# Two PSUM banks per tile in a product-quantised residual block: wider evacuations, moved norms, one-operand VectorE steps

## The chip, the cores and the metric

One core of a Trainium2 chip runs the whole kernel in one launch. The metric is the device time in microseconds; a kernel's time is the median of its runs. The engines are TensorE (PE in the profile, its weight loads PEld), VectorE (DVE), ScalarE (ACT), GpSimd (POOL) and SyncE (SP, which here only issues DMAs).

## The reference

A residual block over x of shape (16, 256, 28, 28), all float32. Two "convolutions" replace the product of patches and weights by a soft look-up: each channel's 3×3 patch is compared with 16 centroids, and the softmax of the negative distances weights a table.

```python
def amm_conv3x3(x, centroids, w_sub):              # centroids (256, 16, 9), w_sub (256, 9, 256)
    patches = conv_general_dilated_patches(x, (3, 3), (1, 1), 'SAME')
    p = patches.reshape(B, C, 9, H*W).transpose(0, 3, 1, 2)
    d = sum(p*p) - 2*einsum('bncs,cks->bnck', p, centroids) + sum(centroids*centroids)
    attn = softmax(-d, axis=-1)
    lut = einsum('cks,cso->cko', centroids, w_sub)
    return einsum('bnck,cko->bno', attn, lut)      # then back to (B, 256, 28, 28)

h = groupnorm(x)                                   # 32 groups
out = relu(bn1(amm_conv3x3(h, centroids1, wsub1)))
out = bn2(amm_conv3x3(out, centroids2, wsub2))
out = out * sigmoid(relu(mean(out) @ w1 + b1) @ w2 + b2)
return x + relu(out + h)
```

## The kernel before

The work is cut into 128 blocks: 2 layers × 16 images × 4 (half of the input channels, half of the image's rows). A block has 128 channels and N = 392 positions. For each block there are these steps:

- `patches` (L338) fetches shifted rows from DRAM (`home1`, `home2`) into the tiles `pt`.
- `logits` (L352), four times (`mm` 0 to 3), computes the scores: 16 small matmuls of 32×32 into four PSUM tiles `lg`, one for each row of the array's 32-row groups (`i`), four column groups in each.
- `exps` (L366) takes exp(2·score) out of PSUM on ScalarE into the tile `e`. In layer 1 the first group of half the blocks goes a longer way (`wide_copy` and what follows), which subtracts the maximum first.
- `num_b` (L412) makes the denominators and the ninth numerator in PSUM (`nb`); `split_b` (ScalarE) and `join_b` (VectorE) take them out, `recip_dve` inverts, `spread` shuffles the reciprocals to where they are needed (`rb`).
- `num_a` (L399), four times, makes the other numerators (`na`, one PSUM tile for each of two row halves `r`). For `mm` 0 and 1 `copy_a` (ScalarE) copies them to SBUF and `scale_q` (GpSimd) scales them there; for `mm` 2 and 3 `scale_a` (VectorE) scales them out of PSUM.
- `product` (L482) multiplies the nine scaled numerators `q` of a block by a weight tile into the accumulator `acc`. A Strassen-like scheme gets the 2×2 block product of an image from seven products; `mix` (GpSimd) forms differences of numerators, `acc_copy`, `acc_add` and `reg_add` assemble the four outputs.
- `norm_out` or `norm_both` applies batch norm on ScalarE; layer 0's result is scattered to DRAM (`to_home2`), layer 1's goes through the gate (`se_hidden`, `se_gate`) and the `finish_` steps to the output.

Nothing is left to a scheduler. Every call is entered by hand with `at(cluster, sub, f, ...)`; the program issues them in order of (cluster, sub), and each engine runs its own in that order. A block starts every two clusters, so an even cluster holds scores (sub 0.1 and 0.2), denominators (1.3), two groups of numerators (1.35) and a product (2.0); an odd one holds scores, two groups of numerators (1.0) and a product. An image takes eight clusters.

```python
at(g + p, 0.1 + 0.1 * q, logits, u, mm)
at(g + p, 0.12 + 0.1 * q, exps, u, mm)
at(g + 2, 1.4, split_b, u)
at(g + 2, 1.45, copy_a, u, mm)
at(g + 12, 0.0, acc_add, l, b, c11, (n, 11))
```

All PSUM tiles share one ring, `p_ring`: eight slots of one bank (512 float32 in each partition). `bank(name)` takes a slot; whoever takes it next waits until all readers of its last owner are done.

Beside the main path some preparation runs once. Group norm of the next image is `gn_stats`, `gn_mean` (with L305, a squaring of two columns), `gn_var` and `gn_apply`. For image 0 the channels of layer 1 are ranked: `code_spread` (L573), `rank_score` (L593), `rank_keep` (L597, which writes 128 scores of 4 bytes each to DRAM), `rank_row`, `rank_make` (L609) and `rank_look`.

Of the kernel before, what the change touches and what calls it, by code (L numbers as in the profile page):

```python
# [17 lines left out]
P = 128  # L18
# [5 lines left out]
N = RT * W  # L24
# [43 lines left out]
def kernel(  # L68
# [28 lines left out]
    p_ring = ctx.enter_context(tc.tile_pool(name="p_ring", bufs=8, space=PSUM))  # L97
# [4 lines left out]

    def bank(name):
        return p_ring.tile([P, 512], F32, tag="ps", name=name)
# [190 lines left out]
    def gn_mean(b, k0=0, n=NB):  # L295
# [9 lines left out]
        nc.vector.tensor_mul(dv[:, :n], dv[:, :n], dv[:, :n])  # L305
# [46 lines left out]
    def logits(u, mm):  # L352
        bs = []
        for i in range(4):
            bk = bank("lg")
# [7 lines left out]
            bs.append(bk)  # L363
        u["lg", mm] = bs

    def exps(u, mm):  # L366
        eg = epool.tile([P, 4, N], F32, tag="e", name="e")
        for i, bk in enumerate(u.pop(("lg", mm))):
            nc.scalar.activation(eg[:, i, :], bk[:, :N], AF.Exp, scale=2.0)  # L369
        u["e", mm] = eg  # L370

    def wide_copy(u, mm):
        eg = epool.tile([P, 4, N], F32, tag="e", name="e")
        for i, bk in enumerate(u.pop(("lg", mm))):
            nc.scalar.copy(eg[:, i, :], bk[:, :N])  # L375
# [23 lines left out]
    def num_a(u, mm):  # L399
        bs = [bank("na") for _ in range(2)]  # L400
        es = u["e", mm]
        for i in range(4):
            for r in range(2):
                nc.tensor.matmul(  # L404
                    bs[r][32 * i : 32 * i + 32, :N],
# [6 lines left out]
    def num_b(u):  # L412
        bs = [bank("nb") for _ in range(2)]
        for mm in range(4):
            es = u["e", mm]
            for i in range(4):
                for r in range(2):
                    nc.tensor.matmul(  # L418
                        bs[r][32 * i : 32 * i + 32, :N],
# [6 lines left out]
    def split_b(u):  # L426
        b0, _ = u["nb"]
# [7 lines left out]
    def join_b(u):  # L435
        _, b1 = u.pop("nb")
# [32 lines left out]
    def copy_a(u, mm):  # L469
        for r, bk in enumerate(u.pop(("na", mm))):  # L470
            u["q", 2 * mm + r] = pair(u, mm)[:, r, :]
            nc.scalar.copy(u["q", 2 * mm + r], bk[:, :N])  # L472

    def scale_a(u, mm):
        rb = u.pop(("rb", mm))
        for r, bk in enumerate(u.pop(("na", mm))):
            u["q", 2 * mm + r] = pair(u, mm)[:, r, :]
            nc.vector.tensor_mul(u["q", 2 * mm + r], bk[:, :N], rb[:, r, :])  # L478
# [94 lines left out]
    def code_spread(o):  # L573
# [8 lines left out]
        nc.vector.tensor_max(csum[:, o : o + 1], csum[:, o : o + 1], m2)  # L582
# [10 lines left out]
    def rank_score(o):  # L593
        nc.vector.tensor_reduce(score[:, o : o + 1], hpads[o], axis=AX.X, op=ALU.max)
        nc.vector.tensor_mul(score[:, o : o + 1], score[:, o : o + 1], posn[:, o : o + 1])

    def rank_keep(o):  # L597
        nc.sync.dma_start(view(d_sc, o * P, [[1, P], [1, 1]]), score[:, o : o + 1])
# [10 lines left out]
    def rank_make(o):  # L609
        row = idx["row"]  # L610
        eq, gt = row[:, 768:1024], row[:, 1024:1280]
        s = score[:, o : o + 1]
        nc.vector.scalar_tensor_tensor(
            eq, row[:, :C], s, row[:, C * (1 + o) : C * (2 + o)], op0=ALU.is_equal, op1=ALU.mult
        )
        nc.vector.scalar_tensor_tensor(gt, row[:, :C], s, eq, op0=ALU.is_gt, op1=ALU.add)
# [286 lines left out]
    for l in range(2):  # L903
        for b in range(B):
# [22 lines left out]
            if l == 0 or b == B - 1:  # L927
                at(g + 11, 1.9, norm_out, l, b, *c12)
                at(g + 11, 1.91, norm_out, l, b, *c22)
                at(g + 12, 0.3, norm_out, l, b, *c11)  # L930
                at(g + 13, 0.3, norm_out, l, b, *c21)
            else:
                for o in range(NB):
                    at(g + 12 + o, 0.3, norm_both, b, o)
            if l == 0:
                for o in range(2):
                    if b == 0:
                        at(g + 12 + o, 0.35, rank_score, o)
# [268 lines left out]
```

## Time and profile before

| | |
|---|---|
| median of 3 runs | 2728.22 us (2721.29 to 2731.6) |
| the profiled execution | 2732.52 us, its span 2731.0 us |
| mean granted TensorE clock | 0.995 |
| PE busy | 2663.6 us (98%), 36984 matmul records |
| VectorE, ScalarE, GpSimd busy | 1718.3, 1445.9, 2075.3 us |
| exps L369 | 1920 of 128×392, 528 ns each |
| copies L472, scalings L478 | 512 each of 128×392, 513 and 554 ns |

A float32 matmul shows as two matmul records and two weight loads. In a line of the profile L369 is line 369 of the kernel; `e<-lg` names the tiles written and read. A timeline line gives start, duration, engine, line, operation, tiles, count and, in brackets, how long the engine stood idle before it and who ended that. The ends of matmuls are modelled, so stages are read from start to start.

### The profile page before, as it was taken

What the parts mean: (1) busy time and instruction counts of PE and PEld (TensorE: products, weight loads), DVE (VectorE), ACT (ScalarE), POOL (GpSimd) and SP (SyncE); (2) the same over time, 40 slices, a digit from 0 to 9 for tenths busy, and PEclk for the clock granted to TensorE, in tenths of its full rate; (3) what the DMA queues carried; (4) which work ended last, traced back from release to release, by engine and by line L of the source; (5) the groups of instructions that cost most, each with busy time, mean ns of one, the idle gap of its engine ahead of it and who ended that gap; (6) DMA issues with size and microseconds to landing.
All of it is one profiled execution on the core that took longest, in us unless ns stands there. A gap on an engine that the chain in (4) does not pass through costs nothing. (4 is left out here: it accounts for less than half of the span.)

```text
span 2731.0 us, 87796 instructions
## 1 busy us (share of the span) xinstructions
PE 2663.6 (98%) x36984; PEld 1293.3 (47%) x36984; DVE 1718.3 (63%) x3943; ACT 1445.9 (53%) x3233; POOL 2075.3 (76%) x1425
## 2 busy tenths in 40 slices
PE   5899999999999999999999999999999999999998
PEld 2444544444444444444444444444444444444444
DVE  4765655566565556655567766666766676766674
ACT  3445444544445554555545555656556656556653
POOL 4856787766887677876678887788887788887787
PEclk9999999999999999999999999999999999999999
DMA  9665667766566666666585555545555445555441
GB/s 198 150 143 159 144 156 197 190 148 129 151 163 160 172 155 140 172 166 160 127 180 119 106 121 121 115 102 116 115 122 125 111 105 115 115 124 125 110 105 57
DMA packets 223624, 374.50 MB, mean 137 GB/s; under 512 B 30633, under 2 KB 194009, under 8 KB 223225
## 3 DMA queue, kind: packets, MB, share of 16 engines
q1 hardware_dynamic: 216280, 334.87, 53.3%
q0 software_dynamic: 6944, 33.95, 3.7%
q8 instruction: 295, 4.83, 0.8%
q14 instruction: 105, 0.85, 0.1%
HBM read 288.93 MB, written 79.80 MB: 135 GB/s over the span
## 5 line engine op out<-in xcount | busy, mean ns | idle before, releaser
L369 ACT ACTIVATE e<-lg 128x392 f32<-128x392 f32 x1920 | 778.2, 528 | 803.9 <-PE lg L357 797.7
L495 POOL TENSOR_TENSOR qp<-qp,qp 128x784 f32<-128x784 f32 x512 | 938.2, 1861 | 26.0 <-DVE qp L478 26.0
L486 PE MATMUL acc<-qp,w_S 128*128 128x392 f32 x2048 | 704.4, 494 | 0.9 <-POOL qp L495 0.9
L467 POOL TENSOR_TENSOR qp<-qp,rb 128x784 f32<-128x784 f32 x256 | 471.5, 1859 | 181.3 <-DVE rb L459 173.5
L357 PE MATMUL lg<-pt,wd 32*32 32x392 f32 x16384 | 541.2, 504 | 21.1 <-DMA pt<-home 16.2
L459 DVE STREAM_SHUFFLE rb<-r 128x392 f32<-128x392 f32 x1024 | 551.7, 603 | 0.0
L486 PEld LDWEIGHTS acc<-qp,w_S 128*128 128x128 f32 x2048 | 386.7, 190 | 299.1 <-issue 17.4
L486 PE MATMUL acc<-qp,w_A 128*128 128x392 f32 x1536 | 521.2, 492 | 0.0
L438 DVE SCALAR_TENSOR_TENSOR r<-nb,kst,r 128x392 f32<-128x392 f32 x128 | 79.8, 624 | 572.9 <-ACT r L429 557.6
L404 PE MATMUL na<-e,cwa 64*32 64x392 f32 x8192 | 412.1, 495 | 9.0 <-issue 9.0
L486 PEld LDWEIGHTS acc<-qp,w_A 128*128 128x128 f32 x1536 | 291.8, 190 | 213.8
L418 PE MATMUL nb<-e,cwb 64*32 64x392 f32 x8192 | 373.8, 496 | 3.9 <-issue 3.4
L467 POOL TENSOR_TENSOR qo<-qo,rb 128x392 f32<-128x392 f32 x128 | 131.0, 1024 | 301.6 <-DVE rb L455 301.4
L357 PEld LDWEIGHTS lg<-pt,wd 32*32 32x32 f32 x16384 | 232.8, 103 | 257.3 <-issue 170.9
L444 DVE RECIPROCAL r<-r 128x392 f32<-128x392 f32 x128 | 331.9, 2593 | 0.0
L478 DVE TENSOR_TENSOR qp<-na,rb 128x392 f32<-128x392 f32 x512 | 253.3, 554 | 68.4 <-PE na L404 58.9
L404 PEld LDWEIGHTS na<-e,cwa 64*32 64x32 f32 x8192 | 147.0, 106 | 236.4 <-ACT e L369 122.0
L418 PEld LDWEIGHTS nb<-e,cwb 64*32 64x32 f32 x8192 | 144.1, 107 | 226.2 <-issue 140.5
L472 ACT COPY qp<-na 128x392 f32<-128x392 f32 x512 | 211.8, 513 | 9.1 <-PE na L404 9.1
L429 ACT ACTIVATE r<-nb,kst 128x392 f32<-128x392 f32 x128 | 87.6, 684 | 105.6 <-PE nb L418 100.8
L375 ACT COPY e<-lg 128x392 f32<-128x392 f32 x128 | 52.9, 501 | 149.8 <-PE lg L357 149.8
L493 POOL TENSOR_TENSOR qo<-qo,qo 128x392 f32<-128x392 f32 x128 | 130.8, 1022 | 1.7
(149 smaller groups left out, 1747.9 us busy)
## 6 DMA issues: line engine op xcount, KB each, us to landing
pt<-home SPq DMA_DIRECT2D x768, 209.0 KB
pt<-home SPq DMA_DIRECT2D x756, 104.5 KB
home<-xpad SPq DMA_DIRECT2D x31, 899.0 KB
xt<-in_x SPq DMA_DIRECT2D x30, 784.0 KB
out_dram<-y SPq DMA_DIRECT2D x32, 392.0 KB
w_S<-d_wS SPq DMA_DIRECT2D x4, 576.0 KB
st<-in_wsub SPq DMA_DIRECT2D x4, 512.0 KB
st<-d_wa SPq DMA_DIRECT2D x16, 128.0 KB
```

Of the source, the lines that this page charges most:

```text
L357: nc.tensor.matmul(bk[32 * c : 32 * c + 32, :N].rearrange("p (r w) -> p r w", w=W), lhsT=wts["wd", u["hh"]][32 * i : 32 * i + 32, mm, c, : ...
L369: nc.scalar.activation(eg[:, i, :], bk[:, :N], AF.Exp, scale=2.0)
L404: nc.tensor.matmul(bs[r][32 * i : 32 * i + 32, :N], lhsT=wts["cwa", u["hh"]][64 * r : 64 * r + 64, mm, i, :], rhs=es[64 * r : 64 * r + 64, ...
L418: nc.tensor.matmul(bs[r][32 * i : 32 * i + 32, :N], lhsT=wts["cwb", u["hh"]][64 * r : 64 * r + 64, mm, i, :], rhs=es[64 * r : 64 * r + 64, ...
L444: nc.vector.reciprocal(u["r"], u["r"])
L459: nc.vector.stream_shuffle(rb[:, r, :], u["r"], mask_of(2 * mm + r))
L467: nc.gpsimd.tensor_tensor(q, q, u.pop(("rb", mm)), ALU.mult)
L472: nc.scalar.copy(u["q", 2 * mm + r], bk[:, :N])
L478: nc.vector.tensor_mul(u["q", 2 * mm + r], bk[:, :N], rb[:, r, :])
L486: nc.tensor.matmul(accs[key][:, :N], lhsT=wl[w][:, k, :], rhs=us["q", k], start=first and n == 0, stop=last and n == len(ks) - 1,)
L493: nc.gpsimd.tensor_tensor(out_u["q", 8], in0["q", 8], in1["q", 8], ALU.subtract)
L495: nc.gpsimd.tensor_tensor(pair(out_u, mm), pair(in0, mm), pair(in1, mm), ALU.subtract)
```

## The change

- The ring has four slots of two banks. `banks(name)` gives both banks as a [128, 2, 512] tile; `bank(name)` gives the first of a slot's two.
- The scores of two rows `i` share a slot, as do the two halves of numerators and of denominators. `exps`, `wide_copy`, `copy_a` and `scale_a` read both banks in one instruction of 784 columns.
- On ScalarE the batch norm of the first half of channels (`norm_out` of c11, `norm_both` of half 0) moves from sub 0.3 to 1.46 of its cluster, and `finish_relu` from 0.9 to 1.46: behind `copy_a` (1.45). What follows image 0's norm (`rank_score`, `rank_keep`, `h0_keep`) moves to 1.91 to 1.93.
- Small VectorE operations of two tensors become operations of one tensor and a per-partition scalar (L305, column by column; L582; L595). `rank_make` compares on VectorE and multiplies and adds on GpSimd; its sum becomes `rank_sum`, a cluster later.
- The score column is copied to 32 columns and transposed in 32×32 blocks, so that `rank_keep` writes four pieces of 128 bytes.

```diff
-    p_ring = ctx.enter_context(tc.tile_pool(name="p_ring", bufs=8, space=PSUM))
+    p_ring = ctx.enter_context(tc.tile_pool(name="p_ring", bufs=4, space=PSUM))
+    def banks(name):
+        return p_ring.tile([P, 2, 512], F32, tag="ps", name=name)
     def bank(name):
-        return p_ring.tile([P, 512], F32, tag="ps", name=name)
+        return banks(name)[:, 0, :]
...
-        nc.vector.tensor_mul(dv[:, :n], dv[:, :n], dv[:, :n])
+        for i in range(n):
+            nc.vector.tensor_scalar_mul(dv[:, i : i + 1], dv[:, i : i + 1], dv[:, i : i + 1])
...
         for i in range(4):
-            bk = bank("lg")
+            if i % 2 == 0:
+                bs.append(banks("lg"))
+            bk = bs[-1][:, i % 2, :]
...
         for i, bk in enumerate(u.pop(("lg", mm))):
-            nc.scalar.activation(eg[:, i, :], bk[:, :N], AF.Exp, scale=2.0)
+            nc.scalar.activation(eg[:, 2 * i : 2 * i + 2, :], bk[:, :, :N], AF.Exp, scale=2.0)
...
-        bs = [bank("na") for _ in range(2)]
+        bs = banks("na")
...
-                    bs[r][32 * i : 32 * i + 32, :N],
+                    bs[32 * i : 32 * i + 32, r, :N],
...
-        bs = [bank("nb") for _ in range(2)]
+        bs = banks("nb")
...
-            nc.scalar.copy(u["q", 2 * mm + r], bk[:, :N])
+        nc.scalar.copy(pair(u, mm), u.pop(("na", mm))[:, :, :N])
...
-            nc.vector.tensor_mul(u["q", 2 * mm + r], bk[:, :N], rb[:, r, :])
+        nc.vector.tensor_mul(pair(u, mm), u.pop(("na", mm))[:, :, :N], rb)
...
-        nc.vector.tensor_max(csum[:, o : o + 1], csum[:, o : o + 1], m2)
+        nc.vector.tensor_scalar_max(csum[:, o : o + 1], csum[:, o : o + 1], m2[:, 0:1])
...
-        nc.vector.tensor_mul(score[:, o : o + 1], score[:, o : o + 1], posn[:, o : o + 1])
+        nc.vector.tensor_scalar_mul(score[:, o : o + 1], score[:, o : o + 1], posn[:, o : o + 1])
+        wide = small.tile([P, 32], F32, name="score_w")
+        nc.vector.tensor_copy(wide, score[:, o : o + 1].to_broadcast([P, 32]))
+        turned = small.tile([P, 32], F32, name="score_t")
+        nc.vector.transpose(turned, wide)
+        idx["turned", o] = turned
     def rank_keep(o):
-        nc.sync.dma_start(view(d_sc, o * P, [[1, P], [1, 1]]), score[:, o : o + 1])
+        nc.sync.dma_start(view(d_sc, o * P, [[32, 4], [1, 32]]), idx["turned", o][::32, :])
...
-        nc.vector.scalar_tensor_tensor(
-            eq, row[:, :C], s, row[:, C * (1 + o) : C * (2 + o)], op0=ALU.is_equal, op1=ALU.mult
-        )
-        nc.vector.scalar_tensor_tensor(gt, row[:, :C], s, eq, op0=ALU.is_gt, op1=ALU.add)
+        nc.vector.tensor_scalar(eq, row[:, :C], s, None, op0=ALU.is_equal)
+        nc.vector.tensor_scalar(gt, row[:, :C], s, None, op0=ALU.is_gt)
+        nc.gpsimd.tensor_tensor(eq, eq, row[:, C * (1 + o) : C * (2 + o)], ALU.mult)
+        nc.gpsimd.tensor_tensor(gt, gt, eq, ALU.add)
+    def rank_sum(o):
...
-                at(g + 12, 0.3, norm_out, l, b, *c11)
+                at(g + 12, 1.46, norm_out, l, b, *c11)
...
-                    at(g + 12 + o, 0.3, norm_both, b, o)
+                    at(g + 12 + o, 0.3 if o else 1.46, norm_both, b, o)
...
-                        at(g + 12 + o, 0.35, rank_score, o)
-                        at(g + 12 + o, 0.6, rank_keep, o)
-                        at(g + 12 + 2 * o, 0.65, h0_keep, o)
+                        at(g + 12 + o, 0.35 if o else 1.91, rank_score, o)
+                        at(g + 12 + o, 0.6 if o else 1.92, rank_keep, o)
+                        at(g + 12 + 2 * o, 0.65 if o else 1.93, h0_keep, o)
...
-                        at(g + 20, 0.9, finish_relu, b, q)
+                        at(g + 20, 1.46, finish_relu, b, q)
...
         at(15 + o, 1.9, rank_make, o)
+        at(16 + o, 1.7, rank_sum, o)
```

More of the change, by code (lines that the diff above doesn't have):

```diff
@@ L362, in logits @@
                 )
-            bs.append(bk)
         u["lg", mm] = bs
@@ L374, in wide_copy @@
         for i, bk in enumerate(u.pop(("lg", mm))):
-            nc.scalar.copy(eg[:, i, :], bk[:, :N])
+            nc.scalar.copy(eg[:, 2 * i : 2 * i + 2, :], bk[:, :, :N])
         u["e", mm] = eg
@@ L418, in num_b @@
                     nc.tensor.matmul(
-                        bs[r][32 * i : 32 * i + 32, :N],
+                        bs[32 * i : 32 * i + 32, r, :N],
                         lhsT=wts["cwb", u["hh"]][64 * r : 64 * r + 64, mm, i, :],
@@ L426, in split_b @@
     def split_b(u):
-        b0, _ = u["nb"]
+        b0 = u["nb"][:, 0]
         r = rpool.tile([P, N], F32, tag="r", name="r")
@@ L435, in join_b @@
     def join_b(u):
-        _, b1 = u.pop("nb")
+        b1 = u.pop("nb")[:, 1]
         r, q, w = u["r"], u["q", 8], u["w"]
@@ L469, in copy_a @@
     def copy_a(u, mm):
-        for r, bk in enumerate(u.pop(("na", mm))):
+        for r in range(2):
             u["q", 2 * mm + r] = pair(u, mm)[:, r, :]
-            nc.scalar.copy(u["q", 2 * mm + r], bk[:, :N])
+        nc.scalar.copy(pair(u, mm), u.pop(("na", mm))[:, :, :N])
     def scale_a(u, mm):
         rb = u.pop(("rb", mm))
-        for r, bk in enumerate(u.pop(("na", mm))):
+        for r in range(2):
             u["q", 2 * mm + r] = pair(u, mm)[:, r, :]
-            nc.vector.tensor_mul(u["q", 2 * mm + r], bk[:, :N], rb[:, r, :])
+        nc.vector.tensor_mul(pair(u, mm), u.pop(("na", mm))[:, :, :N], rb)
     accs = {}
@@ L610, in rank_make @@
         row = idx["row"]
-        eq, gt = row[:, 768:1024], row[:, 1024:1280]
+        eq, gt = row[:, 768:1024], (row[:, 1024:1280] if o else row[:, 1280:1536])
         s = score[:, o : o + 1]
-        nc.vector.scalar_tensor_tensor(
-            eq, row[:, :C], s, row[:, C * (1 + o) : C * (2 + o)], op0=ALU.is_equal, op1=ALU.mult
-        )
-        nc.vector.scalar_tensor_tensor(gt, row[:, :C], s, eq, op0=ALU.is_gt, op1=ALU.add)
+        nc.vector.tensor_scalar(eq, row[:, :C], s, None, op0=ALU.is_equal)
[3 more added lines that the diff above has]
+    def rank_sum(o):
+        gt = idx["row"][:, 1024:1280] if o else idx["row"][:, 1280:1536]
         rf = small.tile([P, 1], F32, name="rf")
```

## The prediction

> **What bounds the kernel now.** I read the page first (part 1), then the waits, then the timeline of two late stretches of work, then the tiles that the diff names.
>
> ```profile
> PE 2663.6 (98%) x36984; PEld 1293.3 (47%) x36984; DVE 1718.3 (63%) x3943; ACT 1445.9 (53%) x3233; POOL 2075.3 (76%) x1425
> ...
> L369 ACT ACTIVATE e<-lg 128x392 f32<-128x392 f32 x1920 | 778.2, 528 | 803.9 <-PE lg L357 797.7
> ```
>
> TensorE is busy 98% of the span; everything else has room. ACT's large idle time ahead of the exps (L369) is ACT waiting for TensorE, so it costs nothing as such. Only time that TensorE loses inside its stages can be won. The timeline shows how much that is. First a short ("odd") cluster of image work in layer 1, then the numerators of a long ("even") one:
>
> ```profile
> 1789.97 2.03 PE L357 MATMUL lg<-pt,wd 32*32 32x392 f32 x64
> ...
> 1790.65 0.63 PEld L357 LDWEIGHTS lg<-pt,wd 32*32 32x32 f32 x31 [0.23 <-issue]
> 1790.95 3.23 ACT L369 ACTIVATE e<-lg 128x392 f32<-128x392 f32 x8 [5.49 <-PE lg L357]
> ...
> 1791.92 1.64 PE L404 MATMUL na<-e,cwa 64*32 64x392 f32 x32
> ...
> 1792.28 0.10 PEld L404 LDWEIGHTS na<-e,cwa 64*32 64x32 f32 x1 [0.18 <-ACT e L369]
> 1792.61 0.24 PEld L404 LDWEIGHTS na<-e,cwa 64*32 64x32 f32 x15 [0.22 <-issue]
> ...
> 1793.49 0.93 PE L486 MATMUL acc<-qo,w_S 128*128 128x392 f32 x2
> ```
>
> ```profile
> 1782.39 1.52 PE L404 MATMUL na<-e,cwa 64*32 64x392 f32 x32
> ...
> 1783.84 0.93 PE L486 MATMUL acc<-qo,w_S 128*128 128x392 f32 x2
> ```
>
> Read start to start. The scores (L357) take 1.95 us in both kinds of cluster (1789.97 to 1791.92). The numerators (L404) take 1.57 us in the odd one (to 1793.49), 1.45 in the even one (1782.39 to 1783.84), for the same 32 matmul records. Product and denominators repeat to the hundredth (6.12 and 2.66 us). So two small losses recur in every cluster. **The second half of the scores** is issued slowly: the records of the first 16 matmuls lie 7 ns apart, those of the second 17 ns, with about 42 ns wherever the next PSUM bank starts, where a load carries a wait for that bank and the matmul before it a signal. Three such steps at 25 ns extra are 0.075 us. **The odd numerators** wait for ACT:
>
> ```profile
> PEld na L404 <- ACT e L369: 122.0, 357, 0.6
> PEld nb L418 <- ACT e L369: 61.7, 94, 1.3
> ```
>
> 357 weight loads of L404 have ACT's exp as their last releaser; the ring hands them the banks that the exps have just read. Most of the 122 us is the change of stage in any case; what the wait really costs is the difference of 1.57 and 1.45.
>
> In layer 0 there is a third loss. The score matmuls need the bank of the last product, which VectorE's addition (L523) releases, and now and then a tiny operation stands before it:
>
> ```profile
> 403.78 2.14 DVE L305 TENSOR_TENSOR gn_dv<-gn_dv 128x2 f32<-128x2 f32 x1
> 404.02 1.86 POOL L467 TENSOR_TENSOR qp<-qp,rb 128x784 f32<-128x784 f32 x1
> ...
> 405.84 0.55 DVE L523 TENSOR_TENSOR hpad<-acc,hpad 128x392 f32<-128x392 f32 x1
> ...
> 406.54 0.53 PE L357 MATMUL lg<-pt,wd 32*32 32x392 f32 x4 [1.15 <-DVE hpad L523]
> ```
>
> A multiplication of two columns takes 2.14 us while POOL runs; the last four score matmuls start at 406.54. By tile it takes 159/300/2139 ns (min/median/max) over 17, and L582, on one column, 1355 and 6711 ns.
>
> [...] L305 and L582 (two SBUF inputs) stretch, L304 (one from PSUM) stays at 145 to 147 ns. [...] the trace has 528 on average and 497 at the start of this stage. [...]
>
> **The change, part by part.**
>
> *Ring.* Eight one-bank slots become four of two banks; `acc`, `gnp`, `sep`, `sqp` now hold a whole one. Counted in order of release, the even cluster's scores get the slots of lg, na, na, acc, the odd one's na, na, nb, acc; numerators and denominators get slots of scores in the same cluster. These are the owners of before, within one bank. One shift: the third row of scores waits for `acc` too, not only the fourth. L523 ends 0.67 us after the scores start, that row goes at 1.04, so nothing is lost, except in the one cluster of eight with two L523 first: some 0.03 us × 32 = +1.0.
>
> *Exps.* 1920 of 392 columns become 960 of 784. The 784-wide forms in the trace (907 ns from SBUF, L805) read SBUF; with two pointer operands 784 columns (L550, 1101) cost 327 more than 392 (L537, 774), which is 0.833 per column. So I add 327 to 497 and take **D = 0.824 us**; bounds 0.80 and 0.91 (L805). It starts 0.027 later, when the second bank is done: 1.015 us after the scores begin, ends at 1.84, seen by TensorE some 0.05 later at 1.89. Before, the second bank came at 1.87 + 0.05. The next starts 0.70 later (0.653 of streaming and the 0.05 that separates exps now) and is seen at 2.61, against 2.71 for the fourth bank before.
>
> *Score issue.* Of three steps inside the second half one stays: 2 × 25 ns = 0.050 us off the stage, ending at 1.905; bounds 0 (the steps are no matter of waits) and 0.06. The first exp (1.89) is just ahead, so it does not eat this. 222 clusters (256 less the 32 above and the first two) × 0.050 = **-11.1**.
>
> *Odd numerators.* The second pair could start 0.68 after the first, at 2.59, and gets its slot at 2.61. Now its first half starts at 2.64, its second at 2.71; with both at 2.61 the last record, and the product with it, comes 0.084 earlier, of which 0.050 is counted: 0.034 × 94 clusters (one odd cluster in four waits little now) = **-3.2**; bounds 0 and -8.
>
> *Numerators' copies and scalings* (L472, L478) go from 512 to 256 each. VectorE: 2 × 0.495 busy becomes about 0.82 + 0.09; 256 × 0.08 = 20 us off an engine that is not the bound: 0, covered by the 6.12 us product.
>
> *Small VectorE operations.* L305 as two operations with a pointer scalar at about 0.17 (L584, 174 ns) costs 0.3, like its undisturbed self, and L582 0.17. What TensorE lost behind them: stretches of 1.97, 1.05, 1.5 and 0.7 us (L305, near 404, 574, 661 and 491 us), 1.7 and 0.7 (L582), 2.1 (L616 near 204 us, whose 256-wide comparison is split, half of it to POOL). That is 9.7; some will turn into other small waits and the wide comparisons may still meet POOL, so I take **-8**; bounds -10 and -3.
>
> *Ranks.* Four POOL operations of about 0.7 us (L752) once. `rank_sum`, which waits for them, stands on VectorE a cluster later, ahead of the spreads of sub 1.8; POOL is past them by then: 0. Score copy and transposition add about 0.3 us to VectorE twice, in slack before L523: 0. The 128 four-byte pieces become four of 128 bytes: SP holds one issue either way, now behind the patches of cluster 12; d_h0's store follows it there. The next patches wait for TensorE anyway ("SPq L343 <- PE lg" is SP's longest wait): 0, bounds -2 and +2.
>
> *Norms and Relu on ACT* move behind the numerators' copies. Now L537 and L550 fill ACT's gap between exps and L429; there no score or product of that cluster or the next is late. Moved, the norm ends near 8.5 us of the 12.2 us cluster, before POOL, at about 11, issues the scatter that reads it; L808 and the store follow a cluster later. 0; if POOL came early, up to 0.8 us × 15 images of waiting in its queue, with the scalings behind it, +3 at most on TensorE.
>
> Sum: +1.0 - 11.1 - 3.2 - 8 = **-21.3**. The profiled execution took 2732.5 us (span 2731.0), 4.3 above the median of 2728.2; it should come to 2711, and the median to 2707.
>
> **Rivals.** *A, nothing in the steady clusters:* signals, not waits, set the issue steps and stay, or the scores end on something else. Then only the small operations pay: 2720. For it: the steps show wait and signal at the same place. Against: in layer 0 clusters with one more semaphore instruction the stage is 0.024 longer. *B, slower:* the wide exp holds two banks until its end, and the denominators and numerators queue behind it. With D = 1.0 the first slot comes at 1.015 + 1.0 + 0.05 = 2.065, 0.11 us behind today's 1.956 in every cluster, the second one at 1.015 + 0.88 + 1.05 = 2.945, in odd clusters 0.22 behind today's (two halves at once allowed for): 128 × 0.11 + 128 × 0.22 = 42, less 8: 2762. It decides from D = 0.915 on (loss 9, about what the small operations win); over 0.95 it is slower by more than 0.5%. For it: L805's 907. Against: PSUM sources are quicker (684 against 774 ns, both with two pointers, L429 and L537). *C, chance in the early part:* from 26 to 342 us TensorE idles 23 us, L404's loads up to 4.8 us at once on "issue", near 16 KB fetches of instructions while the homes are written. A shifted program meets other gaps: ±10 on the forecast.
>
> **Numbers.** A measurement of this kernel can tell about 0.5%, 13.6 us: limits 2714.6 and 2741.9. Forecast 0.62 (0.57 faster, 0.05 same), A 0.18 (0.04, 0.14), B 0.10 (slower), C 0.10 (0.05, 0.05). Faster 0.66, same 0.24, slower 0.10. The forecast's own bounds are 2694 to 2720; with A, C and the mild half of B the range is 2690 to 2734.
>
> **What would show it.** Right: L357 to L404 or L418 at 1.90 to 1.91 us; odd L404 at 1.50 to 1.54; L369 x960 near 0.83 to 0.86; L305 never over 0.25; TensorE's order else unchanged. Wrong: L357 still 1.95 (A); L369 over 0.91 with longer waits of L404 and L418 on it (B); new gaps of TensorE on `acc` or `gnp`.

## The result, and the profile after

The changed kernel takes **2722.59 us** (median of 20 runs, 2712.03 to 2726.09), the kernel before 2728.43 in the same series (20 runs, 2721.29 to 2737.01). The ratio is **0.9973 (0.9963 to 0.9983)**, by which it is some 7 us faster: a third of the 21 us that were forecast, and within the 0.5% that was called no change. The profiled execution took 2724.81 us, its span 2723.3.

The page after, its busy times and the groups that the diff made (columns: line, engine, operation, tiles, shapes, count, busy us, mean ns of one, idle time before and its releaser):

```profile
PE 2656.5 (98%) x36984; PEld 1258.0 (46%) x36984; DVE 1697.9 (62%) x3706; ACT 1369.9 (50%) x1953; POOL 2077.4 (76%) x1429
...
L374 ACT ACTIVATE e<-lg 128x784 f32<-128x784 f32 x960 | 716.7, 831 | 818.4 <-PE lg L363 816.9
...
L483 DVE TENSOR_TENSOR qp<-na,rb 128x784 f32<-128x784 f32 x256 | 236.4, 962 | 59.3 <-PE na L409 56.2
```

ACT has lost 76 us of work and VectorE 20; its 256 scalings (L483) are busy for 0.92 us each, where the prediction put 0.91. TensorE has lost 7.1 us of busy time, about what the kernel gained; neither of the other engines was the bound. The tile `gn_dv` now has its squaring at 202 to 215 ns in every instance, where L305 had gone up to 2139. The same odd cluster of layer 1 that the prediction showed (there from 1789.97), in the timeline after; L363 are the scores, L374 the exps, L409 the numerators, L491 the product:

```profile
1783.60 1.98 PE L363 MATMUL lg<-pt,wd 32*32 32x392 f32 x64
...
1784.65 2.97 ACT L374 ACTIVATE e<-lg 128x784 f32<-128x784 f32 x4 [5.65 <-PE lg L363]
1785.53 0.19 PEld L409 LDWEIGHTS na<-e,cwa 64*32 64x32 f32 x16 [0.67 <-ACT e L374]
...
1786.24 0.19 PEld L409 LDWEIGHTS na<-e,cwa 64*32 64x32 f32 x16 [0.53 <-ACT e L374]
1787.07 0.30 PEld L491 LDWEIGHTS acc<-qo,w_S 128*128 128x128 f32 x2 [0.64 <-issue]
```

Start to start, the scores take 1.93 us instead of 1.95 and the numerators 1.54 instead of 1.57. Both gains are there, and small. The reader is to see what ends each stage: the exp. Before, only the second of the two numerator groups had waited visibly; now each group of numerators waits for one wide exp, at 1785.53 and at 1786.24. The waits say the same:

```profile
PEld na L409 <- ACT e L374: 148.3, 259, 0.7
...
PEld nb L423 <- ACT e L374: 62.3, 94, 1.5
```

Fewer waits (259 instead of 357), longer in sum (148.3 us instead of 122.0).

Medians of the stages over all clusters from 228 us on, first matmul to first matmul of the next stage, from the traces. "Ring alone" and "no ring" are experiments below. Clusters are named by their number modulo 8, with 8 for 0; odd ones have no denominators.

| stage (us) | before | ring alone | no ring | after |
|---|---|---|---|---|
| scores, odd clusters 1, 3 | 1.956 | 1.932 | 1.955 | 1.932 |
| numerators, odd clusters 1, 3 | 1.568 | 1.537 | 1.567 | 1.538 |
| scores, cluster 4, layer 1 | 1.956 | 1.903 | 1.955 | 1.904 |
| scores, cluster 7 (behind a short product) | 1.956 | 1.904 | 1.955 | 1.904 |
| scores, cluster 2 (two additions first), layer 1 | 1.992 | 2.021 | 1.992 | 2.022 |
| scores, cluster 4, layer 0 (group statistics first) | 2.095 | 2.043 | 2.113 | 2.146 |
| scores, cluster 5, layer 1 | 1.956 | 2.242 | 1.955 | 1.933 |
| numerators, cluster 5, layer 1 | 1.567 | 1.478 | 1.567 | 1.536 |

The ring's worth in steady clusters of the changed kernel is the difference of these medians to "no ring", times the clusters of each kind (without cluster 6 of layer 0, whose waits vary): 6.0 us, 3.7 in scores and 2.3 in numerators. The four clusters of layer 0 in which L305 had stretched went from 56.9 to 50.7 us. So 12 us were won in places that can be pointed at, and 7 arrived. The rest was the question.

### The profile page after: what moved, and what is told of

It is laid out like the page before. It is cut to its first block, busy times and chain, and to the rows that moved or that the text cites. A ratio compares the mean times of both kernels' runs of the same rounds, so it can differ in the third digit from the quotient of the medians.

```text
span 2723.3 us, 85963 instructions
## 1 busy us (share of the span) xinstructions
PE 2656.5 (98%) x36984; PEld 1258.0 (46%) x36984; DVE 1697.9 (62%) x3706; ACT 1369.9 (50%) x1953; POOL 2077.4 (76%) x1429
## 4 chain that ended last, share of the span: by engine, by line
PE 90%; DVE 3%; POOL 3%; DMA 2%; issue 1%; SPq 0%; ACT 0%; ACTq 0%; DVEq 0%; POOLq 0%
PE acc L491 47%; PE lg L363 17%; PE nb L423 13%; PE na L409 13%; POOL qp L500 1%; DMA home<-hpad,col 1%; DMA pt<-home 1%; DVE r L449 1%; DVE rb L464 1%; POOL qp L472 0%; SPq L347 0%; DVE r L443 0%; POOL qo L498 0%; DVE qo L446 0%; DVE rb L460 0%
## 5 line engine op out<-in xcount | busy, mean ns | idle before, releaser
L374 ACT ACTIVATE e<-lg 128x784 f32<-128x784 f32 x960 | 716.7, 831 | 818.4 <-PE lg L363 816.9
L491 PE MATMUL acc<-qp,w_S 128*128 128x392 f32 x2048 | 706.8, 495 | 2.3 <-POOL qp L500 2.2
L363 PE MATMUL lg<-pt,wd 32*32 32x392 f32 x16384 | 531.8, 504 | 24.6 <-DMA pt<-home 14.5
L491 PEld LDWEIGHTS acc<-qp,w_S 128*128 128x128 f32 x2048 | 386.8, 191 | 303.3 <-POOL qp L500 11.8
L491 PE MATMUL acc<-qp,w_A 128*128 128x392 f32 x1536 | 521.3, 492 | 0.0
L409 PE MATMUL na<-e,cwa 64*32 64x392 f32 x8192 | 407.9, 498 | 6.6 <-issue 6.5
L491 PEld LDWEIGHTS acc<-qp,w_A 128*128 128x128 f32 x1536 | 292.0, 190 | 213.6
L363 PEld LDWEIGHTS lg<-pt,wd 32*32 32x32 f32 x16384 | 217.3, 103 | 266.3 <-issue 178.8
L483 DVE TENSOR_TENSOR qp<-na,rb 128x784 f32<-128x784 f32 x256 | 236.4, 962 | 59.3 <-PE na L409 56.2
L409 PEld LDWEIGHTS na<-e,cwa 64*32 64x32 f32 x8192 | 127.8, 106 | 253.3 <-ACT e L374 148.3
L477 ACT COPY qp<-na 128x784 f32<-128x784 f32 x256 | 195.4, 820 | 7.3 <-PE na L409 7.3
L380 ACT COPY e<-lg 128x784 f32<-128x784 f32 x64 | 48.9, 815 | 157.1 <-PE lg L363 157.1
```

The source lines that it names most:

```text
L363: nc.tensor.matmul(bk[32 * c : 32 * c + 32, :N].rearrange("p (r w) -> p r w", w=W), lhsT=wts["wd", u["hh"]][32 * i : 32 * i + 32, mm, c, : ...
L374: nc.scalar.activation(eg[:, 2 * i : 2 * i + 2, :], bk[:, :, :N], AF.Exp, scale=2.0)
L409: nc.tensor.matmul(bs[32 * i : 32 * i + 32, r, :N], lhsT=wts["cwa", u["hh"]][64 * r : 64 * r + 64, mm, i, :], rhs=es[64 * r : 64 * r + 64, ...
L477: nc.scalar.copy(pair(u, mm), u.pop(("na", mm))[:, :, :N])
L483: nc.vector.tensor_mul(pair(u, mm), u.pop(("na", mm))[:, :, :N], rb)
L491: nc.tensor.matmul(accs[key][:, :N], lhsT=wl[w][:, k, :], rhs=us["q", k], start=first and n == 0, stop=last and n == len(ks) - 1,)
```

## The experiments

Each kernel was timed in five rounds against the kernel before on the same chip. Ratios are to the kernel before; 0.1% is 2.7 us. Not all rows come from one chip, so they are compared by their ratios and not by their medians.

| kernel | median us | ratio (95%) |
|---|---|---|
| small operations alone | 2721.24 | 0.9987 (0.9977 to 0.9996) |
| ring alone | 2734.85 | 1.0035 (1.0024 to 1.0047) |
| moves and ranks alone | 2713.93 | 0.9956 (0.9940 to 0.9972) |
| all but the ring | 2713.38 | 0.9936 (0.9919 to 0.9952) |
| first exp halved | 2709.03 | 0.9935 (0.9916 to 0.9954) |
| pieces of 128 bytes alone | 2724.71 | 0.9977 (0.9968 to 0.9985) |
| later moves alone | 2728.07 | 0.9986 (0.9975 to 0.9997) |
| first mixed ring | 2753.25 | 1.0080 (1.0067 to 1.0093) |
| first mixed ring and more | 2755.16 | 1.0089 (1.0076 to 1.0102) |
| second mixed ring | 2717.27 | 0.9947 (0.9934 to 0.9960) |
| before, shifted | 2732.39 | 1.0001 (0.9991 to 1.0010) |
| changed, shifted | 2717.75 | 0.9957 (0.9944 to 0.9970) |
| ring alone, shifted | 2740.38 | 1.0042 (1.0024 to 1.0059) |
| all but the ring, shifted | 2714.99 | 0.9945 (0.9923 to 0.9967) |
| second mixed ring, shifted | 2720.43 | 0.9967 (0.9956 to 0.9978) |

### The parts, each alone

Small operations: two edits of the diff on the kernel before, L305 and L582. (The split comparisons of the ranks are in the third part.)

```diff
-        nc.vector.tensor_mul(dv[:, :n], dv[:, :n], dv[:, :n])
+        for i in range(n):
+            nc.vector.tensor_scalar_mul(dv[:, i : i + 1], dv[:, i : i + 1], dv[:, i : i + 1])
```

> The kernel before with the small VectorE operations alone (L305 as two operations with one tensor operand, L582 likewise). My theory: this part wins what the changed kernel shows at the four clusters whose L305 had stretched (3.5, 0.5, 0.9 and 1.3 us there, 6.1 in all), and nothing more for sure, since what it wins before 230 us comes back as other waits: 6 us faster, 2722. The prediction's term: 8 us. Rival: the early stalls move about with any change of the program, by up to 5 us in either direction, so that this part alone may read anything between 1 and 11 us faster; then the stalls before 230 us, not the four clusters, make the difference.

The ring: `p_ring` with four slots of two banks, and every instruction that writes or reads it; nothing else.

```diff
-    p_ring = ctx.enter_context(tc.tile_pool(name="p_ring", bufs=8, space=PSUM))
+    p_ring = ctx.enter_context(tc.tile_pool(name="p_ring", bufs=4, space=PSUM))
```

> The kernel before with the two-bank ring and the wide exps, copies and scalings alone. My theory: score stage 1.93 us in the odd clusters and 1.905 in an undisturbed one, odd numerators 1.54, some clusters after two additions 0.03 to 0.05 us longer: about 3 us faster in the steady clusters, 2725. The prediction's terms for this part: 1.0 - 11.1 - 3.2 = 13.3 us faster, 2715. Rival: the ring does win about 13 us, and the moved norms and ranks of the changed kernel cost 8 to 10 of it.

The rest of the diff: norms, Relu, ranks.

```diff
-                at(g + 12, 0.3, norm_out, l, b, *c11)
+                at(g + 12, 1.46, norm_out, l, b, *c11)
...
-                        at(g + 20, 0.9, finish_relu, b, q)
+                        at(g + 20, 1.46, finish_relu, b, q)
```

> The kernel before with the remaining parts alone: the norms and the Relu moved behind the numerators' copies, and the new rank operations. My theory: no stage of a steady cluster changes by more than 0.01 us; within 3 us of before, of which all lies before 230 us. Rival of the run with the ring alone: 8 to 10 us slower.

The signs were the surprise. The small operations won 3.5 us, near my expectation. **The ring alone is 9.6 us slower** than before, where the prediction had it 13.3 faster. **The moves and ranks, counted at nothing, are 12 us faster.** The parts add up: -0.13, +0.35 and -0.44% make -0.22, against -0.27 measured for all. Neither theory had it right. The rival had the moves eat what the ring wins; it is the other way round.

Where the ring loses is partly in the table: scores of cluster 5 of layer 1 take 2.242 us with the ring alone. The chain that leads there runs through ScalarE's two reads of the denominators (`split_b`), `join_b` on VectorE, and the addition that frees `acc`. In the kernel before, where the scores of that cluster 5 start at 1833.67 (L429 and L431 are `split_b`, L438 the start of `join_b`, L525 the addition):

```profile
1827.96 0.73 ACT L429 ACTIVATE r<-nb,kst 128x392 f32<-128x392 f32 x1
1828.52 0.74 ACT L431 ACTIVATE qo<-nb,kst 128x392 f32<-128x392 f32 x1
...
1828.72 0.63 DVE L438 SCALAR_TENSOR_TENSOR r<-nb,kst,r 128x392 f32<-128x392 f32 x1 [6.57 <-ACT r L429]
...
1834.05 0.54 DVE L525 TENSOR_TENSOR y<-y,acc 128x392 f32<-128x392 f32 x1
```

With the ring alone (L554 is `norm_both`, L809 `finish_relu`, L433 and L435 `split_b`, L442 `join_b`, L529 the addition, L362 the scores):

```profile
1830.02 1.06 ACT L554 ACTIVATE y<-y,bnsh,bnsc 128x784 f32<-128x784 f32 x1
...
1831.04 1.62 ACT L809 ACTIVATE y<-y 128x784 f32<-128x784 f32 x2
...
1832.54 0.69 ACT L433 ACTIVATE r<-nb,kst 128x392 f32<-128x392 f32 x1
...
1833.10 0.70 ACT L435 ACTIVATE qo<-nb,kst 128x392 f32<-128x392 f32 x1
...
1833.83 0.62 DVE L442 SCALAR_TENSOR_TENSOR r<-nb,kst,r 128x392 f32<-128x392 f32 x1 [6.97 <-ACT qo L435]
...
1838.33 2.32 PE L362 MATMUL lg<-pt,wd 32*32 32x392 f32 x64
...
1839.15 0.56 DVE L529 TENSOR_TENSOR y<-y,acc 128x392 f32<-128x392 f32 x1
...
1839.76 0.18 PEld L362 LDWEIGHTS lg<-pt,wd 32*32 32x32 f32 x16 [0.32 <-DVE y L529]
```

Norm and Relu hold ACT until 1832.5, so the denominators leave PSUM late. But they did so before: counted from the scores of the even cluster (1821.48 before, 1826.19 here), ScalarE's first read starts at 6.48 us before and at 6.35 here. The new delay comes behind it. Before, `join_b` starts 0.03 us after the first read has ended, at 7.24; with the ring alone it starts 0.03 us after the second, at 7.64. Reciprocal, shuffles and the addition behind them on VectorE come later with it, and the addition ends 1.38 us after the next scores began instead of 0.92.

This is so in every block. In the nine kernels here in which both halves of the denominators share a slot, all 128 `join_b` start 0.03 us after the second read; in the eight others some 95 of 128 start that close behind the first. The second read ends 0.57 us after the first. No run gives the denominators alone their two slots back, so what this wait costs by itself was not timed.

The second row that waits for `acc` (x16 loads behind L529, where eight slots have x8) adds little. Where the scores of layer 1 end on such an addition, the next stage begins 0.845 us after the addition's end with one row waiting and 0.876 with two (medians): 0.03 us of the 0.29 lost here.

Moving norm and Relu behind `copy_a` lets ScalarE read the denominators earlier and takes the delay away: in the changed kernel the addition ends at 0.67 and the scores take 1.933 us. That is what the moves are for, and the prediction saw neither half of it. The delay costs the ring alone 0.2 us (scores 0.286 longer, numerators 0.089 shorter) in each of 16 clusters, 3.1 us.

### What ends the odd clusters

The changed kernel with the first exp of each cluster cut to half its columns. It leaves the other half of these exponentials out; a copy within SBUF fills their place later with other values.

```diff
+            m = N // 2 if u["w"] > 3 and mm % 2 == i == 0 else N
-            nc.scalar.activation(eg[:, 2 * i : 2 * i + 2, :], bk[:, :, :N], AF.Exp, scale=2.0)
+            nc.scalar.activation(eg[:, 2 * i : 2 * i + 2, :m], bk[:, :, :m], AF.Exp, scale=2.0)
```

> The changed kernel with the first exp of every cluster reading only 196 of its 392 columns a bank (392 in all, as one exp before), and a copy within SBUF behind the fourth exp filling the other half from the last one. Part of the exponentials is so left out. Theory one, the end of the first wide exp sets the end of the odd clusters' scores and the second slot of their numerators: the exp ends 0.33 us earlier, the odd scores fall from 1.931 to 1.905 us and the odd numerators from 1.538 to about 1.45, 0.11 us in each of some 96 odd clusters, 10 us faster than the changed kernel, 2712. Theory two, issue and signals of the scores set both: stages as in the changed kernel, 2722.

The ratio is 0.9935, 10 us under the changed kernel, and theory one holds. The same odd cluster there (L375 are the exps, L414 the numerators):

```profile
1775.04 1.97 PE L363 MATMUL lg<-pt,wd 32*32 32x392 f32 x64
...
1776.04 2.65 ACT L375 ACTIVATE e<-lg 128x392 f32<-128x392 f32 x4 [5.59 <-PE lg L363]
1776.94 0.18 PEld L414 LDWEIGHTS na<-e,cwa 64*32 64x32 f32 x16 [0.64 <-ACT e L375]
```

Scores 1.90 us instead of 1.93; the median of the numerators falls from 1.538 to 1.478 (expected 1.45). In 89 clusters (1, 3 and 5) that is 0.089 each, 7.9 us. It also shows the shortfall of the prediction's step: the first wide exp starts 1.05 us after the scores begin, not 1.015, so its slot is seen free at 1.93, just behind the 1.905 at which the scores could hand over.

### Moves and ranks apart

> The kernel before with the score's 512 bytes written in four pieces of 128 bytes instead of 128 pieces of 4, and nothing moved. Theory one, the small pieces delay TensorE's own instructions: the fetch that took 6.4 us near 154 us takes 1.3, and the numerators that lose 8 us near 170 us lose 1: 8 us faster, 2719. Theory two, it is the place of the store of the first map (450 KB) and of the scores, not their pieces: as before, 2728.

```diff
-        nc.sync.dma_start(view(d_sc, o * P, [[1, P], [1, 1]]), score[:, o : o + 1])
+        nc.sync.dma_start(view(d_sc, o * P, [[32, 4], [1, 32]]), idx["turned", o][::32, :])
```

> The kernel before with the norms and the Relu moved behind the numerators' copies for all images but the first of layer 0, and the ranks as they were. Theory one, the moves themselves are worth nothing as long as the ring has eight slots: no stage changes, within 3 us of before, 2728. Theory two, most of the 12 us won by the kernel with moves and ranks comes from the moved norms: 2718 or less.

```diff
-                at(g + 12, 0.3, norm_out, l, b, *c11)
+                at(g + 12, 1.46 if l or b else 0.3, norm_out, l, b, *c11)
```

(`norm_both` and `finish_relu` as in the change; the pieces come with the copy and the transposition that they need.) The pieces alone give 0.9977, 6.3 us; the later moves 0.9986, 3.8 us. In the kernel before, the numerators of one cluster stop without any semaphore; the timeline has "issue" in brackets, after the idle time:

```profile
172.88 1.56 PE L404 MATMUL na<-e,cwa 64*32 64x392 f32 x18 [0.28 <-issue]
...
178.56 1.54 PE L404 MATMUL na<-e,cwa 64*32 64x392 f32 x10 [4.12 <-issue]
```

With 128-byte pieces the same place reads

```profile
170.00 1.49 PE L404 MATMUL na<-e,cwa 64*32 64x392 f32 x22
...
172.14 0.87 PE L404 MATMUL na<-e,cwa 64*32 64x392 f32 x10 [0.66 <-issue]
```

The stage lasts 10.2 us before, 2.9 here. In the trace's records of instruction fetches, a 16 KB one near 154 us takes 6.4 us before and 1.0 here, and the next comes at 176.1 instead of 169.5. In both kernels the numerators go on 1.5 to 1.6 us after that next fetch has ended, so TensorE probably stands until it has its instructions; that is inferred from these times alone. The 6.4 us fetch lies in the stretch of the small pieces. How they delay it no run shows, and the kernel before in another placement (below) has the small pieces and a fetch of 1.3 us there: what the pieces win is known for this placement alone.

With eight slots the later moves change no stage median by over 2 ns (cluster 6 of layer 0 apart), as theory one said, and the time still fell by 3.8 us. What went were stalls on "issue": 1.4, 1.5 and 0.9 us near 1678, 2171 and 2664 us, and some in layer 0. The Relu's store lies elsewhere in SP's queue, and x's next load with it. That this removed them is argued, not shown: with the ring alone, and the Relu in its old place, they are gone too.

### Other rings

My first idea was that the second row behind `acc` costs most. If so, `acc` should have a bank of its own again. First mixed ring: three slots of two banks for the first three pairs of score rows, numerators and denominators, two of one bank for the last two rows and `acc`.

```diff
+    p_one = ctx.enter_context(tc.tile_pool(name="p_one", bufs=2, space=PSUM))
...
-        return banks(name)[:, 0, :]
+        return p_one.tile([P, 512], F32, tag="po", name=name)
...
+            if mm % 2 and i > 1:
+                bs.append((i, bank("lg").unsqueeze(1)))
```

> The changed kernel with three two-bank slots and two one-bank slots in PSUM: the product, the small sums and the last two rows of the scores use the one-bank slots, so that only the last row of scores waits for the product's bank, as before the change; the last two rows have exps of 392 columns again. Theory one, the ring alone was 10 us slower because its third and fourth rows both wait for the product's bank, so that each late release stops TensorE for half a stage longer and then lets it run at half its clock for some us: the long scores behind late VectorE and ACT (near 203, 600 and 766 us in the changed kernel) shrink to what the kernel with only the moved norms and ranks shows, the stretches at half clock from 10.4 us to about 5, the scores after two additions from 2.02 to 1.99 us: 10 us faster than the changed kernel, 2712. Theory two, those stalls lie where this program's instructions fall: 2722, with stalls at other places.

It was 29 us slower than the changed kernel, a mistake of mine: the product of an odd cluster now takes the bank of the fourth exp, which ends 3.70 us after the scores begin, and waits 0.375 us for it. A version with two more edits shared the mistake:

```diff
-                at(g + (3 if b else 4), 2.1, gn_mean, b + 1)
+                at(g + (3 if b else 4), 1.95 if b else 2.1, gn_mean, b + 1)
...
-        at(15 + o, 1.9, rank_make, o)
+        at(16 + o, 0.06, rank_make, o)
```

> A version meant to beat both: the ring of three two-bank and two one-bank slots; the group means and variances (L301, L315) asked for ahead of the product instead of behind it, so that their VectorE operations no longer stand before the addition that frees the product's bank; the two wide rank comparisons behind the addition instead of before it. Theory one: on top of the 10 us of the mixed ring, 0.15 to 0.2 us in 14 clusters of layer 0 and 3 to 4 us near 190 and 203 us: 2706. Theory two, stalls move elsewhere: as the mixed ring alone, 2712 to 2722.

Its own edits did not pay: the statistics ahead of the product cost 0.27 us in cluster 3 and won 0.07 in cluster 4; the moved comparisons won 1.5 us in one cluster and lost 3.8 in the next.

The second mixed ring computes the one-bank rows last but gives them the third and fourth exp.

```diff
+        for i in (2, 3, 0, 1) if mm % 2 else range(4):
+            if mm % 2 and i < 2:
+                bs.append((i, bank("lg").unsqueeze(1)))
```

> As the first mixed ring (three two-bank slots, two one-bank slots), with the one-bank slots now under the scores that are computed last but whose exps come third and fourth, so that the product's bank comes free before the odd numerators end (in the first mixed ring the product waited 0.35 us for the fourth exp in 115 odd clusters, 40 us in all). Theory one, one row instead of two behind the product's bank is worth the 10 us that the two-bank ring had cost: odd clusters as in the changed kernel, the scores after two additions 0.03 us and those behind STREAM_SHUFFLEs 0.06 us shorter, stretches at half clock about 5 us: 2714, 9 us faster than the changed kernel. Theory two, the cost of the ring lies in the placement of instructions: 2722.

0.9947, 7 us under the changed kernel, with scores of cluster 2 back at 1.992 us. The stall near 203 us looks like the difference of one row and two. In both kernels the two wide rank comparisons (L623, L624 after; L626, L627 here) stand before the addition (L528; L531). After:

```profile
203.03 1.93 DVE L624 TENSOR_SCALAR row<-row,score 128x256 f32<-128x256 f32 x1
...
204.88 0.55 DVE L528 TENSOR_TENSOR hpad<-acc,hpad 128x392 f32<-128x392 f32 x1
...
205.48 0.18 PEld L363 LDWEIGHTS lg<-pt,wd 32*32 32x32 f32 x16 [3.12 <-DVE hpad L528]
205.49 1.33 PE L363 MATMUL lg<-pt,wd 32*32 32x392 f32 x16 [2.41 <-DVE hpad L528]
```

Second mixed ring:

```profile
202.66 1.95 DVE L627 TENSOR_SCALAR row<-row,score 128x256 f32<-128x256 f32 x1
...
204.53 0.56 DVE L531 TENSOR_TENSOR hpad<-acc,hpad 128x392 f32<-128x392 f32 x1
...
205.14 0.15 PEld L366 LDWEIGHTS lg<-pt,wd 32*32 32x32 f32 x8 [1.44 <-DVE hpad L531]
205.14 0.86 PE L366 MATMUL lg<-pt,wd 32*32 32x392 f32 x8 [0.73 <-DVE hpad L531]
```

8 loads wait instead of 16, TensorE idles 0.73 us instead of 2.41, and scores and numerators of the cluster take 4.9 us instead of 8.2. Little of that is the row. The addition ends 2.6 us after the scores began here and 4.2 after: one comparison took 0.38 us here (L626) and 2.01 there (L623). And in the changed kernel the granted clock is 0.50 from 205.8 on, so that its numerators take 2.66 us instead of 1.48. (With the moves and ranks alone, where the addition ended at 3.2, the two stages took 5.5.) `join_b` waits for both reads in the mixed rings too.

**What follows a long stall** is the other half. Near 600 us another late addition on VectorE (`st<-st,sqp`, the preparation of layer 1) delays the scores in the kernel with moves and ranks alone and in the changed kernel. The windows view of both over the scores, the numerators and the product of that cluster (columns: window, its length, busy us and count of PE, PEld, DVE, ACT, POOL, then PEclk, DMA share, GB/s); moves and ranks alone first:

```profile
596.80:600.26 3.46, 2.73 (x65) 0.94 (x65) 3.34 (x12) 2.53 (x7) 3.30 (x3) 1.00 0.81 154
600.26:601.74 1.48, 1.48 (x37) 0.49 (x33) 0.68 (x3) 0.69 (x2) 1.25 (x2) 1.00 0.80 239
```

```profile
597.78:601.83 4.05, 2.65 (x66) 0.86 (x65) 3.93 (x12) 2.25 (x3) 3.60 (x4) 0.99 0.76 141
601.83:604.63 2.80, 2.80 (x41) 0.67 (x33) 1.12 (x2) 0.82 (x1) 1.08 (x2) 0.50 0.85 275
```

The addition ends 2.61 us after the scores began in the first and 3.16 in the second; it is 2.62 in the kernel before and 3.17 with the ring alone, which is the later `join_b` again. TensorE idles 0.73 us in the first, 1.40 in the second, and then the granted clock is 0.50 through all the numerators: they take 2.80 us instead of 1.48. So a stall that the ring makes 0.6 us longer costs 2.2 here. It need not: in the second placement told of below TensorE idles 1.41 us at the same place of the changed kernel, and the clock stays at 1.00 and the numerators at 1.48. In the changed kernel itself an idle time of 1.76 us near 868 us did not bring the half clock either, so the length of one stall does not decide it; what does is not shown. Adding up the surplus of all records that follow each other at half speed (0.65 us instead of 0.34), such stretches cost about 10 us in the changed kernel and 10 with the ring alone, 2 in the kernel before and 3 with all but the ring. In the second placement the four have about 4, 7, 6 and 6: there the changed kernel loses no more to the half clock than the kernel without its ring. So this is a part of the ring's cost in one placement, and not shown to be one in general.

### The version without the ring, and another placement

> The changed kernel without its ring: eight one-bank slots and exps, copies and scalings of 392 columns, with the small operations, the moves and the ranks of the change. If the parts add up (0.9987 for the small operations, 0.9956 for moves and ranks): 0.9943 of before, 2715, and the ring is what takes 8 us back. If instead the parts overlap in the same stalls: 0.996, 2719.

(The changed kernel with the ring's edits taken back.) 0.9936, so the parts add up, and in this placement this is **the version that beats both**: 17 us under the kernel before. Against it the ring, in the company of all the other parts, costs 0.37%.

Programs also differ in when their instructions are fetched, as near 170 us above. 24 multiplications of one column ahead of the first scores shift all that TensorE does later:

```diff
+    ps = bank("gnp")[:, :1]
+    for _ in range(24):
+        nc.tensor.matmul(ps, lhsT=gmat, rhs=gmat[:, :1], start=True, stop=True)
```

> The kernel before with 24 multiplications of one column, whose result nobody reads, put into TensorE's wait for its first patches, so that all later instructions of TensorE lie further back and are fetched at other moments. Theory one, TensorE's stalls without a semaphore depend on when its instructions are fetched: single stalls come and go, the sum moves by up to 5 us in either direction. Theory two, they belong to the work in hand (stores, loads) and stay: within 2 us.

> The changed kernel with the same 24 unread multiplications. As for the kernel before: by up to 5 us in either direction (theory one) or within 2 us of 2722 (theory two). If both shifted kernels keep their distance of 6 to 7 us, the gain doesn't hang on where the instructions happened to lie.

The kernel before did not move (1.0001), but its stalls did: the one of 8 us near 170 us is gone, with the small pieces still there (the fetch near 155 us takes 1.3 us); 5.4 us stand a cluster later, and 6.0 are new near 700 us. The changed kernel fell to 0.9957, by 4.4 us, with intervals that overlap a little. So one placement is not enough for differences of this size, and three more kernels were run in the second.

> The kernel with the ring alone, in the second placement (24 unread multiplications at the start, as in the other shifted kernels). Theory one, the ring itself costs: 1.002 to 1.005 of before again, 2735 to 2745. Theory two, only its first placement was bad: 0.998 to 1.001, as its steady clusters (4 us won) say.

> The changed kernel without its ring, in the second placement. Theory one: 0.992 to 0.995 again, clearly under the changed kernel's 0.9973 and 0.9957 in its two placements. Theory two: 0.996 to 0.998, no better than with the ring.

> The second mixed ring (one row behind the product's bank) in the second placement. Theory one: 0.993 to 0.995, under the changed kernel in both placements. Theory two: anywhere between 0.994 and 0.998, with its stalls at other places than in the first placement.

The ring alone costs in both placements (1.0035, 1.0042); without it the other parts give 0.9936 and 0.9945. The changed kernel has 0.9973 and 0.9957. So the ring takes back 0.37%, 10 us, in the first placement; in the second 0.12%, 3 us, with intervals that overlap widely, so there its loss within the change is not shown.

In the profiled executions what the ring alone costs lies before 228 us, which the kernel before reaches in 228.0 and 231.0 us and the kernel with the ring alone in 236.9 and 236.3. From there to the start of the last cluster it takes 2435.8 and 2433.1 us against 2436.4 and 2437.8: its small steady gains only make up for its stalls. (The two executions of the second pair, 2736.3 and 2737.1 us, lie closer together than the medians do, so this doesn't account for all of the loss there.) In the early part some clusters wait longer for additions, but the time also varies without the ring (220.2 and 228.2 us with all but the ring, 227.9 and 228.4 in the changed kernel); what makes it is open.

The second mixed ring (0.9947, 0.9967) keeps its stages but not its lead over the changed kernel. Its times do not bear out that one row in place of two is worth 7 us, and the traces give that row 0.03 us a stage.

## Why the prediction was wrong, point by point

The bound was right. The direction was right by luck: the ring, which was to win most, lost, and parts that were counted at nothing won. The sum of -21.3 was three times what came. By its own steps:

- **Ring, +1.0.** The step that failed. "L523 ends 0.67 us after the scores start, that row goes at 1.04, so nothing is lost" took the addition's end from an undisturbed cluster of the kernel before and kept it. The ring moves it. With both halves of the denominators in one slot `join_b` comes 0.57 us later in some 95 of 128 blocks, and additions behind its chain end later: at 1.37 us instead of 0.93 in clusters 5 of layer 1 with the norms in their old place, at 1.09 instead of 0.75 in clusters 8 of layer 1, at 3.16 instead of 2.62 near 600 us. The prediction counted the owners of the slots and not this wait. The second waiting row costs the 0.03 us it said, but in more clusters than its 32 (2.113 to 2.146 behind group statistics). Ring alone: 9.6 and 11.5 us slower in two placements, in spite of its steady gains. How much of this total the later `join_b` makes stays open.
- **Exps, D = 0.824.** Right: 831 ns on average, against 497 of the stage's first exp and 327 for 392 more columns, and rival B's deciding point of 0.915 was never near. Its start was 0.04 us too early.
- **Score issue, -11.1.** The mechanism was right, to 2 ns where nothing else ends the stage: 1.956 to 1.904. Why the second half is issued more slowly at all (17 ns apart against 7) no trace shows. The size was off. "The first exp (1.89) is just ahead, so it does not eat this" is the failed term: it ends at 1.88 and is seen at 1.93, which leaves 0.024 in odd clusters; clusters 2 and 8 wait for the addition instead (+0.030, +0.010). Over all it came to -3.7.
- **Odd numerators, -3.2.** 0.030 each instead of 0.034; -2.3.
- **Small VectorE operations, -8.** L305 did what was said: its four stretched clusters lost 6.2 us. Its two operations take 0.21 us each and not 0.17, which shows where it had not stretched (2.095 to 2.113). Timed alone L305 and L582, which made up 7.6 of the 9.7 us of waiting that the term counted, won 3.5 (1.1 to 6.3). The rest of the term, the wide comparisons, failed. That an operation of one tensor keeps its time beside POOL was the author's estimate. L305's two did (202 to 215 ns in all 32 instances, 24 of them with POOL at work); the multiplication of nine columns by a constant in `code_spread` (L584, 173 and 174 ns before; L589 after), also of one tensor, took 6245 and 904 ns in the changed kernel, and both ended 0.03 us after an operation of POOL. The comparisons took 2.01 and 1.93 us while POOL worked, against 1.30 and 1.98 before. One took 0.38 in the one instance that met no POOL work at all (first mixed ring and more, near 205 us), but 0.38 also with POOL at work (second mixed ring, L626). What makes one stretch is not shown.
- **Ranks, 0 (-2 to +2).** Failed: the pieces alone won 6.3 us in the one placement in which they were timed. The copy and the transposition took 0.18 and 0.21 us each time, about the 0.3 that was said. I weighed SP's queue, and not the fetches of instructions, 295 of 16 KB in the kernel before. Rival C named this resource and gave it no sign.
- **Norms and Relu, 0.** Right for eight slots, stage by stage, though the time fell by 3.8 us; wrong for four, where they are what keeps `acc` in time. The step costed two edits apart that only work together.

So a net close to rival A's 2720 came by luck out of three errors: the ring with its exps, issue and numerators was counted at -13.3 and costs 10 us in the change in one placement and 3, not clear of noise, in the other; ranks and moves were counted at 0 and are worth -12; the small operations won 3.5 instead of 8. What stays open: how the ring's cost divides into the later `join_b`, other waits and half clock, what makes the early part longer, and how small pieces delay a fetch.

## What to carry to other kernels

Widening a buffer's slot ties its halves together: who takes it waits for the latest reader of either half, and here the reader of one half (`join_b`) came to wait for the reader of the other, 0.57 us in some 95 of 128 blocks. Before counting the gain, list every instruction that reads or releases a slot, in the disturbed clusters as well as the typical one, and see in the trace what each then waits for. When a stage is won by 50 ns, the next thing in line has to be known to better than that. Time each part of a change alone: here a loss and a gain, both counted with the wrong sign, hid each other.

## What the runs showed of the hardware

- TensorE's granted clock fell to 0.50 after an idle of 1.40 us, and numerators of 1.48 us took 2.80; after 0.73 us, and after 1.41 us at the same place in another placement, it stayed at 1.00, and after 1.76 us elsewhere in the same kernel.
- A score stage of layer 1 that ends on an addition hands over 0.845 us after it with 8 loads waiting and 0.876 with 16.
- A 784-column exp out of two PSUM banks takes 831 ns, two of 392 took 1056; in latency nothing is won, since the two overlapped: the second bank was free at 1.92 us before and both are at 1.93 now.
- A wait with its signal between 32×32 matmuls of the scores costs about 25 ns of issue: two of three steps gone are 0.052 us.
- TensorE stood without any semaphore for up to 4.1 us at once and some 8 us in one stage, and went on 1.5 us after a 16 KB fetch of instructions had ended; 24 extra multiplications moved such stalls about. One kernel's time went down by 4 us with them, with intervals that overlap a little, the other's not at all.
